# Layer 1's V in four second-level products instead of seven, q's combinations on VectorE, q's averages in other tiles

## The chip, the cores and the metric

The kernel runs on one core of a Trainium2 chip. The metric is the device time of one execution in microseconds, as the median of several runs. All data are float32. TensorE (PE) multiplies into PSUM, VectorE (DVE) and ScalarE (ACT) read PSUM and SBUF, GpSimd (POOL) works on SBUF alone, and SyncE (SP) issues most of the transfers.

## The reference

Eight images of 512 channels and 32 x 32 positions (N = 1024) pass through two attention layers.

```python
# layer 0: group norm of 32 groups, 8 heads of 64
h = group_norm(x, norm_w, norm_b)
q, k, v = split_heads(einsum('oc,bchw->bohw', qkv_w, h) + qkv_b)
attn = softmax(einsum('bhnd,bhmd->bhnm', q, k) / sqrt(64))
x = x + einsum('oc,bchw->bohw', proj_w, heads(attn @ v)) + proj_b
# layer 1: norm over the whole image, one head of 512
n = (x - mean(x)) * rsqrt(var(x) + 1e-5) * gn_gamma + gn_beta
q, k, v = wq @ n + bq, wk @ n + bk, wv @ n + bv
attn = softmax(q.T @ k * 512**-0.5)
x = x + wo @ (v @ attn.T) + bo
```

In layer 1 the kernel folds wq with wk, and wv with wo, into single weights (`wqk1`, `wvo1`). It then computes one "q", to be multiplied with the image itself, and one "V" from the image itself. The change lies in these two products.

## The kernel before

**Strassen steps.** Nearly every matrix product is a Strassen step: the operands are cut into quarters (A11 to A22, B11 to B22), combinations of them (S1 to S4, T1 to T4) are formed, and seven products of half the size replace eight. The seven are (A11, B11), (A12, B21), (S1, T1), (S2, T2), (S3, T3), (A22, T4) and (S4, B22). A product can itself be cut a second time in the same way, into seven products of quarter size; its operands then need their own combinations, called "twice" in the code. `PAIRS` and `REST` name which first-level products are taken together in a bank: `PAIRS` holds (A12, B21), (S1, T1), (S4, B22) and (A22, T4), `REST` holds (A11, B11), (S2, T2) and (S3, T3).

**Two forms of a product.** `by_two_steps` cuts only the four products of `PAIRS` a second time. They run in 14 steps (0 to 13, two groups of seven in turn), and the three others follow as larger matmuls that accumulate in one bank, in six "line" steps (14 to 19). `seven_by_two_steps` cuts all seven: groups z (two products) and w (one) in 14 steps, some additions between results, then groups c and d (two products each) in 14 more, then more additions. Each step is a few matmuls into one bank of PSUM and one read of it, a copy on ScalarE where the result is fresh, an addition on VectorE where it isn't. A bank is written again some steps later, after its read.

**Which form is where.** In layer 1, q is cut in all seven in images 0 to 6 (`make_q_twice`), and V too (`make_v_all`, L1778, with the matmuls at L1786). In the last image, 7, q has a form of its own (`make_q`), and V is `make_v_twice` (L1047, matmuls at L1055, line steps through L783), which is `by_two_steps` with the four of `PAIRS`.

**Order.** The instruction orders of PE, ScalarE and VectorE are as written in the code (`manual_schedule`). GpSimd's and SP's queues are ordered by the framework from the order of the code and what is ready. Each queue runs in its order, so an instruction that waits holds all that is behind it. Work of other kinds is put between steps by `at_steps`: `hooks` and `hooks_v` map a step's number to what is issued after it, in q and in V.

**What stands at the hooks of q (images 0 to 6).** The norm of layer 1 is needed only at the end of q. `both_halves` is seven tiny GpSimd operations. `mean_of_all` (step 5) and `deviation` (step 9) each do a small matmul with `in_sample` (L305), which averages over the partitions, and write its result into half a PSUM tile that `room(name, 0)` takes from `spares[0]`, here the second bank of z's tile "o". VectorE reduces it (L307), and GpSimd or VectorE goes on. `untaken` and `bias` (step 12) are eight tiny operations on VectorE, and the additions at the end of the first half (L712) need them.

**What stands at the hooks of V.** `onto_first` (step 2) adds the bias to q's first quarter on ScalarE. `finish_q` (L1776) forms q's four combinations S1 to S4, eight adds of 128x512, and `halve_a("S1")` (L520) the four combinations of S1's quarters: in images 0 to 6 both on GpSimd at step 2, in image 7 on VectorE at steps 5, 7, 9, 11 and 17. `measure_later` are the statistics of the image after next (ScalarE, four operations each, from the tiles x_stat), at steps 14, 17, 19, 21 of q and then of V, and `both_halves` for them at step 26 of V. They exist in images 0 to 5.

**After V.** The scores stage (`line`, `twice`) multiplies q's parts with the image. It first forms further quarters (A12, S3, T3 on VectorE at its steps 2, 5, 8; S4 and A22 on GpSimd), and sums of V's quarters follow on GpSimd (L1963).

**Weights.** A weight's second-level combinations are computed once, in image 0, and stored in device memory (`make_twice`). `WeightTwice` loads them back for each image, one tile of up to 512 KB for each entry of `TWICE`. For `wvo1` there are four entries, 2, 2, 2 and 1 products.

Of the kernel before, what the change touches and what calls it, by code (L numbers as in the profile page):

```python
# [46 lines left out]
P = 128  # L47
# [18 lines left out]
def two_attention_blocks(  # L66
# [35 lines left out]
    def tile2(name):  # L102
        return tpool.tile([P, 2, HALF], FP, tag="t", name=name)
# [451 lines left out]
    PAIRS_Q = [[("A12", "B21"), ("S4", "B22")], [("S1", "T1"), ("A22", "T4")]]  # L555
    PAIRS = [[("A12", "B21"), ("S1", "T1")], [("S4", "B22"), ("A22", "T4")]]
    REST = [[("A11", "B11"), ("S2", "T2")], [("S3", "T3")]]
    TWICE = {"wqk1": PAIRS + REST, "wvo1": PAIRS + REST}

    class WeightTwice:  # L560

# [117 lines left out]
    def seven_by_two_steps(multiply, at, z, c, w, bias, name):  # L679

        def group(tag, products, use_of):
            line, single = (banks(t, f"ps_{t}{tag}_{name}") for t in "so")
            spares.append(single[:, 1, :])  # L690
            line, single = line[:, 0, :], single[:, 0, :]
            for bank, x, y, start, fresh, r, t in [
                (line, "A11", "B11", True, True, 0, 0), (single, "A12", "B21", True, False, 0, 0),
                (line, "S2", "T2", False, True, 0, 1), (single, "S1", "T1", True, True, 1, 1),
                (line, "S3", "T3", False, False, 1, 1), (single, "S4", "B22", False, False, 0, 1),
                (line, "A22", "T4", False, True, 1, 0),
            ]:
                multiply(bank, products, x, y, start)
                tiles, always = use_of
                to = at(tiles, r, t)  # L700
                of = bank[:, : len(products) * 2 * P].rearrange("p (i q) -> p i q", i=to.shape[1])
                if fresh and not always:
                    nc.scalar.copy(to, of)
                else:
                    nc.vector.tensor_tensor(to, of, to, ALU.add)
                yield

        def plus(to, x, y, by=None):
            if by is None:
                nc.vector.tensor_tensor(to, x, y, ALU.add)  # L710
            else:
                nc.vector.scalar_tensor_tensor(to, x, by, y, ALU.add, ALU.add)  # L712

        def in_order(order, **groups):
            for n in order:
                next(groups[n])
                yield

        spares.clear()
        first = dict(z=group("z", REST[0], (z, False)), w=group("w", REST[1], (w, False)))  # L720
        yield from in_order("zzwzwzwzwzwzww", **first)
        for k in range(2):
            plus(z[k][:, 1, :], z[k][:, 0, :], z[k][:, 1, :], bias and bias(k, 0))
        for k in range(2):
            plus(w[k], w[k], z[k][:, 1, :], bias and bias(k, 1))
        spares.clear()
        c_of, d_of = [("S1", "T1"), ("A22", "T4")], [("A12", "B21"), ("S4", "B22")]
        second = dict(c=group("c", c_of, (c, False)), d=group("d", d_of, (z, True)))
        yield from in_order("ccdcdcdcdcdcd", **second)
        next(second["d"])  # L730
        for k in [1, 0]:
            plus(z[k][:, 1, :], z[k][:, 1, :], c[k][:, 0, :])
        for k in range(2):
            both = w[k].unsqueeze(1).to_broadcast([P, 2, HALF])
            nc.gpsimd.tensor_tensor(c[k], c[k], both, ALU.add)
        yield
        spares.clear()
# [233 lines left out]
    def flat(t):  # L971
        return t.rearrange("p h n -> p (h n)")
# [71 lines left out]
    def columns_of(w):  # L1044
        return lambda i, name: w.parts[0][name][:, :, i * P : (i + 1) * P]
# [100 lines left out]
    def layer0(bs, qs, ks, vs, b, norm_next, ending, begun):  # L1146
# [69 lines left out]
        if b == 0:  # L1216
# [16 lines left out]
            hooks[7].append(p0.finish)  # L1233
            at_steps(together(*pairs_qk(w, 1, bs, qs, ks, b)), hooks)
            steps = []
            for name, ns in [("v0", range(2)), ("p0", range(2)), ("wqk1", range(4)), ("wvo1", range(2, 4))]:
                of = [columns_of(of) for of in waiting if of.name == name]
                steps += make_twice(name, ns, of[0] if of else None)
            for n, step in enumerate(steps):
                at_units.setdefault(3 + 3 * n // 2, []).append(step)  # L1240
        else:
            ps[0], = begun
            accs[units[0][:2]] = ps[0]
# [321 lines left out]
    def attention1(xs, norm, ready, b, at_values, norms):  # L1565
# [170 lines left out]
            (of["A11"], of["A21"]), (of["A12"], of["A22"]) = ([halves(t) for t in ts] for ts in qs)  # L1736
        else:
            hooks = {
                0: [norm.both_halves], 5: [norm.mean_of_all], 9: [norm.deviation],
                12: [norm.untaken, lambda: biases.append(norm.bias())],  # L1740
                16: [lambda: twice_w.append(WeightTwice("wvo1"))],
            }
            if b + 2 < B:
                later = []

                def load_later(i):
                    if not i:
                        norms[b + 2] = norm0([later, None], b + 2)
                    norms[b + 2].xs[i] = [tile2(f"x_{b + 2}_{i}{half}_stat") for half in range(2)]
                    for half in range(2):  # L1750
                        nc.sync.dma_start(norms[b + 2].xs[i][half], quarter_of(x, b + 2, i, half))

                def measure_later(n):
                    norms[b + 2].moments(n // 2, n % 2, n % 2 == 0)

                for i in range(2):
                    hooks.setdefault(10 * i, []).append(lambda i=i: load_later(i))
                for n in range(4):
                    hooks.setdefault([14, 17, 19, 21][n], []).append(lambda n=n: measure_later(n))
                    hooks_v.setdefault([14, 17, 19, 21][n], []).append(lambda n=n: measure_later(n + 4))  # L1760
                hooks_v[26] = [lambda: norms[b + 2].both_halves()]
                at_values[5] = [lambda: norms[b + 2].mean_of_all()]
                at_values[7] = [lambda: norms[b + 2].deviation()]
            at_steps(make_q_twice(w), hooks)
# [1 line left out]

        w = next_weight("wvo1")

        def finish_q(n, engine):
            of[f"S{n}"] = halves(tile2(f"s{n}_q_{b}"))  # L1770
            x, y, op = {
                1: ("A21", "A22", ALU.add), 2: ("S1", "A11", ALU.subtract),
                3: ("A11", "A21", ALU.subtract), 4: ("A12", "S2", ALU.subtract),
            }[n]
            for k in range(2):
                engine.tensor_tensor(of[f"S{n}"][k], of[x][k], of[y][k], op)  # L1776

        def make_v_all(w):  # L1778


            parts = twice_w[0].all(columns_of(w))

            def multiply(bank, products, x, y, start):
                for i, (a, v) in enumerate(products):
                    for u in range(2):
                        nc.tensor.matmul(  # L1786
                            bank[:, (2 * i + u) * P : (2 * i + u + 1) * P],
                            twice_b[v][y][:, u * P : (u + 1) * P], parts[a][x],
                            start=start and i == u == 0, stop=True, skip_group_check=True,
                        )  # L1790

            def at(tiles, r, t):
                both = tiles[t] if len(tiles[t].shape) == 2 else flat(tiles[t])
                return both.rearrange("p (m o) -> p m o", o=2 * P)[:, :, r * P : (r + 1) * P]

            z, c = ([tile2(f"{n}_v_1_{b}_{t}") for t in range(2)] for n in "zc")
            u = halves(tile2(f"w_v_1_{b}"))
            v_of.update({
                (0, 0): [t[:, 0, :] for t in z], (1, 0): [t[:, 1, :] for t in z],
                (0, 1): [t[:, 0, :] for t in c], (1, 1): [t[:, 1, :] for t in c],  # L1800
            })
            return seven_by_two_steps(multiply, at, z, c, u, None, f"v_1_{b}")

        v_of = {}
        if last:
            v_pairs = places_v(f"1_{b}")
            for n in range(1, 5):
                hooks_v.setdefault(2 * n + 3, []).append(lambda n=n: finish_q(n, nc.vector))
            hooks_v[17] = [lambda: halve_a("S1")]
            at_steps(make_v_twice(w, twice_w[0], bs, twice_b, v_pairs, f"v_1_{b}"), hooks_v)  # L1810
            v_of.update({(n, i): [t[:, i, :] for t in v_pairs[n]] for n in range(2) for i in range(2)})
        else:
            for n in range(1, 5):
                hooks_v[2].append(lambda n=n: finish_q(n, nc.gpsimd))
            hooks_v[2].append(lambda: halve_a("S1", None, nc.gpsimd))
            at_steps(make_v_all(w), hooks_v)


        ps = [[[tile2(f"p_1_{b}_{j}{k}{i}") for i in range(2)] for k in range(2)] for j in range(2)]
# [103 lines left out]
        def halve_t3():  # L1923
# [12 lines left out]
        halve_a("S4", None, nc.gpsimd)  # L1936
        halve_a("A22", None, nc.gpsimd)
        svs = {f"S{n}": tile2(f"s{n}_v_1_{b}") for n in range(1, 5)}
        quarter_v = [
            [[t.rearrange("p (u o) -> p u o", u=2) for t in v_of[n, i]] for i in range(2)] for n in range(2)  # L1940
        ]
        v_parts = [
            {
# [763 lines left out]
```

## Time and profile before

| | before |
|---|---|
| median of 3 runs | 2817.36 us (2816.91 to 2820.29) |
| profiled execution | 2814.56 us |
| its span, first to last instruction | 2812.1 us |
| one image (first matmul of V in image 0 to that in image 1: 342.21 to 686.71) | 344.5 us |
| granted TensorE clock | 0.999 |

The profile is of one execution. Groups are by source line, engine, operation and tiles, with count, busy time, mean duration and the idle time of the engine before them. PE is the matmul part of TensorE, PEld its weight loads, which overlap. In the list of stretches each row gives the stretch, its length, the busy time of each engine with the count of its instructions in brackets, the granted clock, the share of DMA and GB/s. In the lists in order of time each row gives the start, the time to the end of the row's last instruction, the engine, the line and the tiles, and in square brackets the idle time before with what ended it.

### The profile page before, as it was taken

The page shows a single profiled execution, that of the slowest core. Times are in us where ns is not written, and L with a number is a line of the kernel's source. Part 1 is how long each engine was busy: PE and PEld are TensorE (multiplying, and loading weights), DVE is VectorE, ACT ScalarE, POOL GpSimd, SP SyncE. Part 2 cuts the span into 40 slices and gives each one's busy share as a digit, 9 for nine tenths or more (in the row PEclk, how much of TensorE's full clock was granted, in tenths as well). Part 3 has the DMA queues.
Part 4 walks back from the last instruction along what each step waited for, and adds up shares of the span by engine and source line. Part 5 has one row for each costly group of instructions (what it writes and reads, how often), then busy time and mean ns, then how long its engine had stood idle before and what let it go on. Part 6 is the DMA issues. An engine that isn't in the chain of part 4 may idle for free.

```text
span 2812.1 us, 42413 instructions
## 1 busy us (share of the span) xinstructions
PE 2771.6 (99%) x16570; PEld 1648.4 (59%) x16570; DVE 2197.6 (78%) x2993; ACT 1197.3 (43%) x1939; POOL 741.0 (26%) x710
## 2 busy tenths in 40 slices
PE   9999999999999999999999999999999999999999
PEld 5437774377643776437764477645676356763375
DVE  6787687876878768887688877877778877788877
ACT  3453443625346153462535524255342653326622
POOL 0001470015600265002640036400463005520021
PEclk9999999999999999999999999999999999999999
DMA  7555513255142551326422264322633236240101
GB/s 256 198 145 198 217 57 139 58 207 194 57 139 58 210 191 65 135 62 229 165 103 96 76 226 153 123 84 70 239 139 139 69 92 240 86 168 30 36 27 39
DMA packets 117552, 366.50 MB, mean 130 GB/s; under 512 B 25388, under 2 KB 26188, under 8 KB 110944
## 3 DMA queue, kind: packets, MB, share of 16 engines
q1 hardware_dynamic: 90576, 301.26, 31.1%
q10 hardware_dynamic: 26768, 62.46, 6.7%
q8 instruction: 132, 2.16, 0.3%
q14 instruction: 76, 0.62, 0.1%
HBM read 259.85 MB, written 79.99 MB: 121 GB/s over the span
## 4 chain that ended last, share of the span: by engine, by line
PE 93%; DVE 3%; issue 2%; DMA 1%; ACT 0%; ACTq 0%; SPq 0%; POOL 0%; DVEq 0%; POOLq 0%
PE ps_o L1185 15%; PE s L1136 14%; PE ps_o L2025 10%; PE ps_l L1860 5%; PE ps_l_qk L1034 5%; PE ps_s L1843 4%; PE ps_s L1860 4%; PE ps_s_qk L1027 3%; PE ps_l_v L783 3%; PE ps_l_p L768 3%; PE ps_o_qk L1027 2%; PE ps_s_v L1055 2%; PE ps_s_p L1092 2%; PE ps_s_two L2155 2%; PE ps_o_v L1055 2%
## 5 line engine op out<-in xcount | busy, mean ns | idle before, releaser
L940 ACT ACTIVATE p<-s 128x1024 f32<-128x1024 f32 x505 | 516.2, 1024 | 310.2 <-PE s L1136 303.4
L942 DVE TENSOR_TENSOR acc<-acc,p 128x1024 f32<-128x1024 f32 x384 | 469.2, 1222 | 64.0 <-ACT p L940 55.7
L1136 PE MATMUL s<-qk_back,qk_back 64*64 64x512 f32 x3528 | 457.4, 590 | 0.0
L1185 PE MATMUL ps_o<-p,v_back 64*64 64x512 f32 x3528 | 455.3, 589 | 0.0
L537 POOL TENSOR_TENSOR B_twice_p<-o 128x512 f32<-128x512 f32 x14 | 20.9, 1494 | 1070.7 <-DVE o L1205 1070.7
L1185 PEld LDWEIGHTS ps_o<-p,v_back 64*64 64x64 f32 x3528 | 134.9, 133 | 243.6 <-issue 239.8
L1136 PEld LDWEIGHTS s<-qk_back,qk_back 64*64 64x64 f32 x3528 | 132.6, 133 | 245.6 <-issue 216.5
L2025 PE MATMUL ps_o<-t_p,s_v 128*128 128x512 f32 x384 | 169.6, 596 | 0.0
L1834 ACT ACTIVATE p<-p,factor 128x512 f32<-128x512 f32 (+1 forms) x112 | 84.5, 780 | 113.3 <-DVE p L1870 86.4
L537 POOL TENSOR_TENSOR B_twice<-x 128x512 f32<-128x512 f32 x23 | 35.6, 1549 | 358.6 <-DVE x L1447 177.2
L2025 PEld LDWEIGHTS ps_o<-t_p,s_v 128*128 128x128 f32 x384 | 71.8, 190 | 88.4 <-issue 88.0
L942 DVE TENSOR_TENSOR acc<-p,p 128x1024 f32<-128x1024 f32 x57 | 69.7, 1223 | 45.7 <-ACT p L940 45.7
L1870 DVE TENSOR_TENSOR p<-ps_l,p 128x512 f32<-128x512 f32 x136 | 91.5, 688 | 17.8 <-PE ps_l L1860 16.1
L1848 ACT COPY p<-ps_s 128x512 f32<-128x512 f32 x96 | 53.1, 588 | 114.3 <-PE ps_s L1843 114.3
L1034 PE MATMUL ps_l_qk<-t,w_qk 128*128 128x512 f32 x224 | 100.3, 595 | 0.3
L641 ACT COPY c_q<-ps_s_qk 128x512 f32<-128x512 f32 x56 | 32.7, 583 | 140.7 <-PE ps_s_qk L1027 140.7
L373 POOL TENSOR_TENSOR rstd<-rstd,minus_half 128x4 f32<-128x4 f32 (+1 forms) x16 | 12.9, 806 | 285.0 <-DVE rstd L372 285.0
L1831 POOL TENSOR_TENSOR acc<-acc,p 128x512 f32<-128x512 f32 x48 | 83.5, 1740 | 13.3 <-ACT p L1834 10.8
L1870 DVE TENSOR_TENSOR p<-ps_s,p 128x512 f32<-128x512 f32 x112 | 74.7, 684 | 7.8 <-PE ps_s L1860 7.7
L1034 PEld LDWEIGHTS ps_l_qk<-t,w_qk 128*128 128x128 f32 x224 | 42.0, 190 | 56.3 <-issue 50.2
L661 DVE SCALAR_TENSOR_TENSOR c_q<-ps_l_qk,vec,c_q 128x512 f32<-128x512 f32 x56 | 40.8, 749 | 34.2 <-PE ps_l_qk L1034 33.8
L659 DVE TENSOR_TENSOR c_v<-ps_l_v,c_v 128x512 f32<-128x512 f32 x64 | 42.7, 689 | 31.3 <-PE ps_l_v L783 31.2
(780 smaller groups left out, 6077.0 us busy)
## 6 DMA issues: line engine op xcount, KB each, us to landing
x<-in_x SPq DMA_DIRECT2D x64, 512.0 KB, 9.2
qk_back<-kept_qk SPq DMA_DIRECT2D x56, 512.0 KB, 6.2
w_qk<-stored_qk SPq DMA_DIRECT2D x14, 1792.0 KB, 8.6
fold<-acc SPq DMA_DIRECT2D x56, 256.0 KB, 3.0
qk_twice<-stored_qk_twice ACTq DMA_DIRECT2D x28, 512.0 KB
kept_v<-c_v SPq DMA_DIRECT2D x28, 512.0 KB
kept_qk<-c_q SPq DMA_DIRECT2D x28, 512.0 KB, 3.3
kept_qk<-c_k SPq DMA_DIRECT2D x28, 512.0 KB, 3.5
```

What stands on the lines that cost most here:

```text
L940: nc.scalar.activation(p, s, AF.Exp, scale=factor)
L942: nc.vector.tensor_tensor(acc, first, p, ALU.add)
L1027: nc.tensor.matmul(bank[:, i * 2 * P : (i + 1) * 2 * P], parts[a][x], twice_b[v][y], start=start and i == 0, stop=True, skip_group_check=True,
L1034: nc.tensor.matmul(bank, of(i, a)[:, k, :], bs[v][:, k, :], start=start and k == 0, stop=k == 1, skip_group_check=True,)
L1055: nc.tensor.matmul(bank[:, (2 * i + u) * P : (2 * i + u + 1) * P], twice_b[v][y][:, u * P : (u + 1) * P], parts[a][x], start=start and i = ...
L1136: nc.tensor.matmul(s[cols, j, :], ks[pair][k0 // HALF][rows, k0 % HALF : k0 % HALF + HD], qs[pair][g][rows, :], start=True, stop=True,)
L1185: nc.tensor.matmul(o[cols, half, :], vs[n][kt % 4 // 2][rows, h, c0 : c0 + HD], p[rows, j, :], start=kt == 0, stop=kt == NT - 1,)
L1834: nc.scalar.activation(p, p, AF.Exp, scale=norm.factor)
L1843: nc.tensor.matmul(bank, bs[v][:, k, t * P : (t + 1) * P], of[a][k], start=a == "A11" and k == 0, stop=k == 1, skip_group_check=True,)
L1860: nc.tensor.matmul(bank[:, u * 2 * P : (u + 1) * 2 * P], v[y][:, u * P : (u + 1) * P], a[x], start=start and u == 0, stop=True, skip_group ...
L1870: nc.vector.tensor_tensor(at(r, t), bank, at(r, t), ALU.add)
L2025: nc.tensor.matmul(bank, v_parts[kt // 2][a][:, kt % 2, c * P : (c + 1) * P], p_parts[kt // 2][b][:, kt % 2, cols], start=fresh and kt == ...
```

## The change

V takes one form in all images: `make_v_all` goes, and `make_v_twice` runs with the four products of `PAIRS`. q stays with all seven. `wvo1` loses its `REST` combinations: they are no longer computed in image 0, nor loaded. The steps that compute stored combinations in image 0 are spaced two units apart instead of one and a half.

q's combinations S1 to S4 are formed by VectorE in all images, in images 0 to 6 after steps 7, 9, 11 and 13 of V, and S1's quarters by VectorE after step 15. The statistics in V move from steps 14, 17, 19, 21 (of 28) to 5, 8, 11, 14 (of 20), and their `both_halves` to step 17.

In q, `spares` now holds two half tiles for each group, in the order z's "o", z's "s", w's "o", w's "s". The mean moves from step 5 to step 7 and goes into w's "s"; the deviation moves from step 9 to step 11 and stays in z's "o"; `untaken` and `bias` move from 12 to 13.

```diff
-    TWICE = {"wqk1": PAIRS + REST, "wvo1": PAIRS + REST}
+    TWICE = {"wqk1": PAIRS + REST}
...
         def group(tag, products, use_of):
             line, single = (banks(t, f"ps_{t}{tag}_{name}") for t in "so")
-            spares.append(single[:, 1, :])
+            spares.extend([single[:, 1, :], line[:, 1, :]])
...
-            for name, ns in [("v0", range(2)), ("p0", range(2)), ("wqk1", range(4)), ("wvo1", range(2, 4))]:
+            for name, ns in [("v0", range(2)), ("p0", range(2)), ("wqk1", range(4))]:
...
-                at_units.setdefault(3 + 3 * n // 2, []).append(step)
+                at_units.setdefault(3 + 2 * n, []).append(step)
...
             hooks = {
-                0: [norm.both_halves], 5: [norm.mean_of_all], 9: [norm.deviation],
-                12: [norm.untaken, lambda: biases.append(norm.bias())],
+                0: [norm.both_halves], 6: [lambda: spares.insert(0, spares[3])], 7: [norm.mean_of_all],
+                10: [lambda: spares.pop(0)], 11: [norm.deviation],
+                13: [norm.untaken, lambda: biases.append(norm.bias())],
                 16: [lambda: twice_w.append(WeightTwice("wvo1"))],
...
-                    hooks_v.setdefault([14, 17, 19, 21][n], []).append(lambda n=n: measure_later(n + 4))
-                hooks_v[26] = [lambda: norms[b + 2].both_halves()]
+                    hooks_v.setdefault([5, 8, 11, 14][n], []).append(lambda n=n: measure_later(n + 4))
+                hooks_v[17] = [lambda: norms[b + 2].both_halves()]
...
-        def finish_q(n, engine):
+        def finish_q(n):
...
             for k in range(2):
-                engine.tensor_tensor(of[f"S{n}"][k], of[x][k], of[y][k], op)
-
-        def make_v_all(w):
...
-        if last:
-            v_pairs = places_v(f"1_{b}")
-            for n in range(1, 5):
-                hooks_v.setdefault(2 * n + 3, []).append(lambda n=n: finish_q(n, nc.vector))
-            hooks_v[17] = [lambda: halve_a("S1")]
-            at_steps(make_v_twice(w, twice_w[0], bs, twice_b, v_pairs, f"v_1_{b}"), hooks_v)
...
-        else:
-            for n in range(1, 5):
-                hooks_v[2].append(lambda n=n: finish_q(n, nc.gpsimd))
-            hooks_v[2].append(lambda: halve_a("S1", None, nc.gpsimd))
-            at_steps(make_v_all(w), hooks_v)
+                nc.vector.tensor_tensor(of[f"S{n}"][k], of[x][k], of[y][k], op)
+
+        v_pairs = places_v(f"1_{b}")
+        for n in range(1, 5):
+            hooks_v.setdefault(2 * n + (3 if last else 5), []).append(lambda n=n: finish_q(n))
+        hooks_v.setdefault(17 if last else 15, []).append(lambda: halve_a("S1"))
+        at_steps(make_v_twice(w, twice_w[0], bs, twice_b, v_pairs, f"v_1_{b}"), hooks_v)
```

More of the change, by code (lines that the diff above doesn't have):

```diff
@@ L1775, in finish_q @@
             for k in range(2):
-                engine.tensor_tensor(of[f"S{n}"][k], of[x][k], of[y][k], op)
-        def make_v_all(w):
[L1781 to L1802, printed above, removed]
@@ L1804, in attention1 @@
-        v_of = {}
-        if last:
-            v_pairs = places_v(f"1_{b}")
-            for n in range(1, 5):
-                hooks_v.setdefault(2 * n + 3, []).append(lambda n=n: finish_q(n, nc.vector))
-            hooks_v[17] = [lambda: halve_a("S1")]
-            at_steps(make_v_twice(w, twice_w[0], bs, twice_b, v_pairs, f"v_1_{b}"), hooks_v)
-            v_of.update({(n, i): [t[:, i, :] for t in v_pairs[n]] for n in range(2) for i in range(2)})
-        else:
-            for n in range(1, 5):
-                hooks_v[2].append(lambda n=n: finish_q(n, nc.gpsimd))
-            hooks_v[2].append(lambda: halve_a("S1", None, nc.gpsimd))
-            at_steps(make_v_all(w), hooks_v)
+                nc.vector.tensor_tensor(of[f"S{n}"][k], of[x][k], of[y][k], op)
@@ L1938, in attention1, with halves_of @@
         svs = {f"S{n}": tile2(f"s{n}_v_1_{b}") for n in range(1, 5)}
+        def halves_of(n, i):
+            return [t[:, i, :] for t in v_pairs[n]]
         quarter_v = [
-            [[t.rearrange("p (u o) -> p u o", u=2) for t in v_of[n, i]] for i in range(2)] for n in range(2)
+            [[t.rearrange("p (u o) -> p u o", u=2) for t in halves_of(n, i)] for i in range(2)] for n in range(2)
         ]
```

## The prediction

> **What bounds the kernel now.** I read the page first, then what TensorE (PE) waited for, then the stretches of layer 1 in image 0 beside those of the last image, then the instructions in order of time.
>
> ```profile
> PE 2771.6 (99%) x16570; PEld 1648.4 (59%) x16570; DVE 2197.6 (78%) x2993; ACT 1197.3 (43%) x1939; POOL 741.0 (26%) x710
> ```
>
> PE is busy for 2771.6 of 2812.1 us, so there are two ways to gain: less PE work, or fewer of the 40 us in which PE stands. The list of PE's waits says where those are.
>
> ```profile
> PE ps_oc_v L1786 <- DVE c_v L705: 18.9, 7, 2.7
> PE ps_oz_q L305 <- DVE z_q L705: 6.1, 7, 0.9
> PE ps_oz_q L305 <- ACT z_q L703: 5.4, 7, 0.8
> ```
>
> Columns: us in total, times, longest. All three occur once in each of images 0 to 6, and all lie in stages that the change touches: the first in V, the others at the two averages inside q. The stretches (span, then busy us by engine): q, V and scores of image 0, then V and scores of image 7, which already runs the code that images 0 to 6 are given.
>
> ```profile
> 318.03:342.21 24.18, 22.41 (x103) 18.74 (x102) 14.97 (x32) 11.90 (x28) 3.77 (x13) 1.00 0.89 326
> 342.21:367.11 24.90, 22.20 (x197) 22.00 (x196) 17.77 (x23) 13.04 (x30) 20.75 (x21) 1.00 0.21 75
> 367.11:411.39 44.28, 44.28 (x175) 32.52 (x174) 39.44 (x49) 17.79 (x28) 31.63 (x26) 1.00 0.17 60
> 2690.80:2713.67 22.87, 22.87 (x161) 21.63 (x160) 18.14 (x33) 4.68 (x8) 6.29 (x8) 1.00 0.00 1
> 2713.67:2757.62 43.95, 43.95 (x173) 32.68 (x172) 32.99 (x48) 17.99 (x28) 11.18 (x8) 1.00 0.00 1
> ```
>
> The reader is to see that V with four products twice (22.87 us) has more PE work than V with seven (22.20 busy) and is still shorter than it (24.90), for it has no hole. Where the hole comes from, image 0 in order of time (VectorE, GpSimd, PE):
>
> ```profile
> 351.69 3.28 DVE L710 TENSOR_TENSOR z_v<-z_v 128x512 f32<-128x512 f32 x2
> 354.89 3.43 DVE L710 TENSOR_TENSOR w_v<-w_v,z_v 128x512 f32<-128x512 f32 x2
> 358.24 0.68 DVE L705 TENSOR_TENSOR c_v<-ps_oc_v,c_v 128x512 f32<-128x512 f32 x1
> ...
> 354.38 3.39 POOL L1776 TENSOR_TENSOR s_q<-z_q 128x512 f32<-128x512 f32 x2
> ...
> 358.97 1.16 PE L1786 MATMUL ps_oc_v<-wvo_twice,T_twice 128*128 128x128 f32 x8 [2.71 <-DVE c_v L705]
> ```
>
> The four L710 adds of V take 6.7 us while GpSimd forms q's combinations; the same two-operand line takes 1.29 us for two in q (343.21), when GpSimd is idle. The read of ps_oc_v stands behind them, and PE behind that read.
>
> [...] 3.28 against 1.29 us above, while VectorE's adds with one PSUM input keep 0.68 us beside the same GpSimd work. [...]
>
> **The change part by part**, per image, images 0 to 6.
>
> *V's matmuls.* Removed: 98 matmuls of 128 columns. The trace has two PE instructions for each and 8 in 0.893 us (352.53 to 353.42), so 196 x 0.1117 = 21.9 us. Added: 56 of that kind (12.5) and 24 of 256 columns (48 x 0.2158 = 10.4): 22.87, which is what image 7 measures. Cost +1.0 us of work; the hole of 2.7 and some 0.3 us of small change go. V without a new wait: 22.87 - 24.90 = **-2.03 us**.
>
> *q's combinations to VectorE.* Eight adds of 128x512; in image 7 they cost 1.28 us for two. GpSimd loses 12 us and the S1 quarters. VectorE loses in V the four L710 adds and one z += c pair (8 us). Does VectorE stay ahead of PE? Offsets from V's start, 0.893 us a step for steps 0 to 13, then 1.727. S1 (step 7) needs c_q += w_q on GpSimd, which ends at 349.05, offset 6.84: S1 is done by about 8.1, and the next read of a bank is due at 8.2. S2, S3, S4 behind steps 9, 11, 13 end at 11.0, 13.5, 14.7. Covered by PE: nothing.
>
> *ScalarE.* The second half of the statistics moves from steps 14 to 21 of 27 to steps 5 to 14 of 20: 1.73 us each, between copies of 0.58. Copy 6 then ends at offset 8.4, and PE writes that bank again at 8.93; copy 7 at 8.9 against 9.82. Tight, covered. Their data is there: SP issued those four loads by 324.4 and they land in 9.6 us.
>
> *S1's quarters, step 15.* This is the weak place. Image 7 has them at step 17 and with GpSimd just idle again; here they come ahead of the read for step 16, which PE needs at step 18 (offset 19.42). Adds of steps 14 and 15 end near 17.1. GpSimd takes S4's and A22's quarters as soon as S4 is there (in image 7 at 2704.44, 0.2 us after it), here from 14.7, or from 16.7 behind the seven tiny operations of the statistics, for 6.5 us or more. The same four quarters with GpSimd idle (image 7) and beside just those GpSimd quarters (image 0):
>
> ```profile
> 2711.03 0.41 DVE L520 TENSOR_TENSOR S_twice<-s_q 128x256 f32<-128x256 f32 x1
> 2711.48 0.42 DVE L520 TENSOR_TENSOR S_twice<-S_twice,s_q 128x256 f32<-128x256 f32 x1
> ...
> 376.45 0.41 DVE L520 TENSOR_TENSOR spare<-s_q 128x256 f32<-128x256 f32 x1
> 376.89 0.83 DVE L520 TENSOR_TENSOR spare<-spare,s_q 128x256 f32<-128x256 f32 x1
> 377.65 0.94 DVE L520 TENSOR_TENSOR spare<-s_q 128x256 f32<-128x256 f32 x1
> 378.52 0.94 DVE L520 TENSOR_TENSOR spare<-s_q,spare 128x256 f32<-128x256 f32 x1
> ```
>
> So 1.5 us against 2.9. Undisturbed: 17.1 + 1.5 + 0.7 (the read) = 19.3 to 19.5, PE waits 0.1 at most. Disturbed: 17.3 to 17.6 + 2.9 + 0.7 = 20.9 to 21.2, PE waits **1.5 us** at step 18. I take that; bounds 0.1 and 2.6 (other adds in steps 13 to 15 slowed as well). V: -2.03 + 1.5 = **-0.5 us**.
>
> *q's averages.* Before, each writes into the tile that the step just ahead of it filled, and waits for that tile's reader. From 321.91 + 0.43 to 323.49, and from 326.16 to 327.42, PE spends 1.15 and 1.26 us, 2.57 with the slower start behind each; in image 7 an average costs 0.14 + 0.09. After, the first goes into w's score tile, read one step earlier (PE gets there 1.29 us after step 5's end, ScalarE's second copy ends at 1.15), the second into z's other tile, read two steps earlier. The spread on GpSimd needs 1.6 us from the first average, and four steps give 2.6. Gain 2.57 - 0.46 = 2.1. But the deviation now comes only two steps ahead of the second group: untaken waits for GpSimd's power and begins some 0.4 us later against PE, and behind it stands the read that PE already waits for at ps_oc_q (0.3 us, the hole ahead of 334.34). Hence **-1.7 us**; bounds -2.1 and -0.9 (one average still waiting).
>
> *Scores.* GpSimd has no c_v += w_v (5.2 us) after V, VectorE no z += c: 44.28 falls towards image 7's 43.95. Taken **-0.3**, bounds 0 and -0.33.
>
> *Edits at nothing.* Two loads (768 KB) fewer per image on ScalarE's queue, and in image 0 twelve adds of 0.28 us, three loads, two stores and a wider spacing of such steps: layer 0 is hidden behind PE, which is busy 107.77 of 107.77 us in units of image 1; uncovered, 3.4 us once. SP's weight loads keep their releasers; fewer buffers are held, so no tile comes free later.
>
> **Sum.** -0.5 - 1.7 - 0.3 = -2.5 us (2.53 unrounded) x 7 = -17.7 us. The profiled execution took 2814.56 us, so 2796.9; the median of the runs shown lies 2.8 above it, which gives 2799.7.
>
> **Rivals.**
> A (the forecast): both holes go, S1's quarters cost 1.5 us. 2799.7. Against it: GpSimd's order there is not in the trace.
> B: GpSimd's quarters miss S1's (they come earlier, or later because of order: in image 0 they stood behind c_v += w_v although S4 was there). -2.03 + 0.1 - 1.7 - 0.33 = -3.96 x 7: 2789.6.
> C, slower: S1's quarters block behind long GpSimd instructions. The row of spare<-c_q,c_q has 2574 ns for one quarter beside a 128x1024 GpSimd add, and spare<-spare,c_q 2454. With two such and two of 0.94 the four last 6.9 us, PE waits about 5.5 at step 18: V +3.5, q -1.7, sum +1.8 x 7 = +12.6: 2830.0. It decides from a halving of 5.2 us on (a wait of 3.7 eats V's 2.03 and q's 1.7). Against it: those long adds should be over at offset 6.84.
> D: VectorE is late in both stages: q -0.9, V +0.4 (a wait of 2.4), scores 0: -0.5 x 7 = -3.5: 2813.9.
>
> **How the numbers follow.** A 0.52, B 0.25, D 0.15, C 0.08. Of D I count 0.05 as faster, 0.10 as within 0.2% (5.6 us, what a measurement of this kernel can tell). Faster 0.82, same 0.10, slower 0.08. The range holds A with its bounds and B, and leaves out C and most of D: 2787 to 2813.
>
> **What would show it.** PE's waits without ps_oc_v and without the two at L305; V near 24.4 us, with a hole of 1.5 just ahead of the last two line steps, released by VectorE's add onto c_v, and S1's quarters at 0.8 to 0.9 us just before it. V at 22.9 means B. A wait on ScalarE's copies at steps 10 or 11 would say that the statistics were moved too early; holes over 3.7 us in V, or a longer q, that the forecast is wrong.

## The result, and the profile after

The changed kernel takes 2797.93 us (median of 4 runs, 2797.44 to 2798.8) against 2817.14 us before (4 runs, 2813.59 to 2820.29): a ratio of 0.9933, 95% interval 0.9915 to 0.995. The forecast was 2799.7. Its profiled span is 2797.1 us, 15.0 less than before.

The page, engines:

```profile
PE 2772.4 (99%) x16318; PEld 1645.5 (59%) x16318; DVE 2147.5 (77%) x3023; ACT 1186.7 (42%) x1911; POOL 598.2 (21%) x612
```

PE is busy for 0.8 us more than before, and GpSimd for 143 us less. So all of the gain lies in time in which PE stood, that is, waited with nothing to do. (The page counts a matmul at a lower clock as busy for as long as it takes: in the profile before PE is busy for all of the 3.41 us from 179.64 with 20 matmuls, at a clock of 0.50, and for all of the next 3.41 us with 36, at 1.00.) PE's waits (total, times, longest):

```profile
PE ps_l_v L783 <- DVE c_v L659: 9.3, 7, 1.4
PE ps_oc_q L1697 <- DVE c_q L705: 2.6, 7, 0.4
PE ps_l_qk L1034 <- DVE c_k L661: 2.1, 2, 1.4
PE ps_sum L1315 <- DVE acc L1307: 1.4, 1, 1.4
...
PE ps_sc_q L1697 <- ACT c_q L703: 0.7, 1, 0.7
```

The three waits shown of before are gone. In place of V's 18.9 us stand 9.3 us at the line steps, and nothing at L305. q, V and scores of image 0 after the change, as stretches:

```profile
316.17:338.41 22.24, 21.87 (x104) 18.92 (x103) 14.78 (x32) 11.90 (x28) 3.16 (x12) 1.00 0.86 319
338.41:363.16 24.75, 23.38 (x162) 21.54 (x161) 19.03 (x30) 11.55 (x26) 14.09 (x18) 1.00 0.21 75
363.16:407.30 44.14, 44.14 (x173) 32.59 (x172) 31.58 (x47) 17.79 (x28) 17.90 (x16) 1.00 0.18 62
```

So q went from 24.18 to 22.24, V from 24.90 to 24.75, scores from 44.28 to 44.14. Nearly all of the gain per image is q's. V kept its length although its old hole went, for a new one stands in it. In order of time, image 0, VectorE, GpSimd and PE:

```profile
355.57 0.78 DVE L520 TENSOR_TENSOR S_twice<-s_q 128x256 f32<-128x256 f32 x1
356.38 0.83 DVE L520 TENSOR_TENSOR S_twice<-S_twice,s_q 128x256 f32<-128x256 f32 x1
357.14 0.94 DVE L520 TENSOR_TENSOR S_twice<-s_q 128x256 f32<-128x256 f32 x1
358.00 0.94 DVE L520 TENSOR_TENSOR S_twice<-s_q,S_twice 128x256 f32<-128x256 f32 x1
358.87 1.27 DVE L659 TENSOR_TENSOR c_v<-ps_l_v,c_v 128x512 f32<-128x512 f32 x2
...
355.34 1.59 POOL L520 TENSOR_TENSOR S_twice<-s_q 128x256 f32<-128x256 f32 x2
356.89 0.90 POOL L520 TENSOR_TENSOR S_twice<-S_twice,s_q 128x256 f32<-128x256 f32 x1
357.76 0.90 POOL L520 TENSOR_TENSOR A_twice<-c_q,c_q 128x256 f32<-128x256 f32 x1
...
359.60 3.72 PE L783 MATMUL ps_l_v<-w_wvo,t 128*128 128x256 f32 x16 [1.37 <-DVE c_v L659]
```

This is the order that the forecast assumed: GpSimd's S4 and A22 quarters begin 0.2 us before S1's on VectorE, both engines slow down (a quarter takes 0.78 to 0.94 us on VectorE, 0.41 where GpSimd is idle, and 0.90 on GpSimd, 0.72 once VectorE's are over), the two reads of the bank stand behind them, and PE waits 1.37 us behind the first read.

Over seven images, by stage lengths: q -12.4 us, V -2.7 (1.4 of it in image 5 alone, see the last section), scores -0.8. Outside them, layer 0 of image 0 is 2.6 shorter. A new wait at L1034 (ps_l_qk) gives back 1.3 in image 4 and 0.7 in image 0. That makes -16.5; VectorE's last operation is 16.7 us earlier. The end of the kernel behind it is 1.7 longer in this profile. That end takes 4.2 to 6.0 us in the twelve profiles, and what sets it was not followed up.

### The profile page after: what moved, and what is told of

It reads as the page before. It is cut to its first block, busy times and chain, and to the rows that moved or that the text cites. A ratio compares the mean times of both kernels' runs of the same rounds, so it can differ in the third digit from the quotient of the medians.

```text
span 2797.1 us, 41715 instructions
## 1 busy us (share of the span) xinstructions
PE 2772.4 (99%) x16318; PEld 1645.5 (59%) x16318; DVE 2147.5 (77%) x3023; ACT 1186.7 (42%) x1911; POOL 598.2 (21%) x612
## 4 chain that ended last, share of the span: by engine, by line
PE 91%; DVE 5%; POOL 1%; issue 1%; ACT 1%; DMA 1%; ACTq 0%; SPq 0%; DVEq 0%; POOLq 0%
PE ps_o L1185 15%; PE s L1136 15%; PE ps_o L1995 10%; PE ps_l L1827 5%; PE ps_l_qk L1034 5%; PE ps_s L1810 4%; PE ps_l_v L783 4%; PE ps_s L1827 4%; PE ps_s_qk L1027 3%; PE ps_l_p L768 3%; PE ps_o_qk L1027 2%; PE ps_s_v L1055 2%; PE ps_s_p L1092 2%; PE ps_s_two L2125 2%; PE ps_o_v L1055 2%; PE ps_o_two L2125 1%
## 5 line engine op out<-in xcount | busy, mean ns | idle before, releaser
L659 DVE TENSOR_TENSOR c_v<-ps_l_v,c_v 128x512 f32<-128x512 f32 x120 | 79.2, 686 | 44.8 <-PE ps_l_v L783 44.7
L1034 PE MATMUL ps_l_qk<-t,w_qk 128*128 128x512 f32 x224 | 100.3, 595 | 2.3 <-DVE c_k L661 2.1
L641 ACT COPY c_v<-ps_s_v 128x512 f32<-128x512 f32 x90 | 52.7, 585 | 91.1 <-PE ps_s_v L1055 91.1
L1034 PEld LDWEIGHTS ps_l_qk<-t,w_qk 128*128 128x128 f32 x224 | 42.0, 190 | 58.3 <-issue 50.2
```

What stands on the lines that cost most here:

```text
L1034: nc.tensor.matmul(bank, of(i, a)[:, k, :], bs[v][:, k, :], start=start and k == 0, stop=k == 1, skip_group_check=True,)
```

## The experiments

All were compared with the kernel before; the edits are against the changed kernel unless said otherwise.

### S1's quarters two steps later

```diff
-        hooks_v.setdefault(17 if last else 15, []).append(lambda: halve_a("S1"))
+        hooks_v.setdefault(17, []).append(lambda: halve_a("S1"))
```

> The changed kernel with one edit: S1's quarters stand after step 17 of V, behind both reads that PE's last two line steps need, instead of after step 15. Theory (VectorE's quarters of S1 are slowed by GpSimd's quarters and hold the read that step 18 needs): the wait of PE at ps_l_v (9.3 us in total, 1.4 each, some 1.7 with the slower starts) goes, the quarters themselves stay slow (about 0.9 each), V takes 22.9 to 23.1 us, and the kernel 7 x 1.4 to 1.7 less than the changed one: 2786 to 2788. Rival (VectorE has too much to do at V's end, so PE waits a little later): V falls to 22.9 but the first products of the scores stage wait for their bank by 1 us or more, and the time stays at 2795 to 2799.

Measured: 2787.38 us (2786.44 to 2787.71), ratio 0.9889, 0.9874 to 0.9904. V is 23.11 or 23.12 in all seven images, without a wait. VectorE in image 0:

```profile
359.12 0.69 DVE L659 TENSOR_TENSOR c_v<-ps_l_v,c_v 128x512 f32<-128x512 f32 x1 [1.03 <-PE ps_l_v L783]
359.73 0.90 DVE L520 TENSOR_TENSOR S_twice<-s_q 128x256 f32<-128x256 f32 x1
360.67 0.83 DVE L520 TENSOR_TENSOR S_twice<-S_twice,s_q 128x256 f32<-128x256 f32 x1
361.42 0.94 DVE L520 TENSOR_TENSOR S_twice<-s_q 128x256 f32<-128x256 f32 x1
```

Three of the quarters are as slow as before the edit, but the read that PE needs is now ahead of them. The place costs, not the slowness by itself. One number of a hook is worth 1.64 us of V in images 0 to 5 and 1.28 in image 6. The median falls by 10.5 us, more than half of what all of the change brought.

### S1's quarters on GpSimd

```diff
-        hooks_v.setdefault(17 if last else 15, []).append(lambda: halve_a("S1"))
+        if last:
+            hooks_v.setdefault(17, []).append(lambda: halve_a("S1"))
+        else:
+            hooks_v[7].append(lambda: halve_a("S1", None, nc.gpsimd))
```

> The changed kernel with one edit: in images 0 to 6 S1's quarters are formed by GpSimd, behind step 7, as soon as S1 is there and in GpSimd's idle stretch before the statistics; VectorE has none of them. Theory: no wait at ps_l_v, V 22.9 to 23.1 us, 2786 to 2788; S2's two adds on VectorE may be slowed from 1.3 to 2.2 us by GpSimd, which is covered. Rival (whatever GpSimd does in V costs VectorE and so PE): a wait of 0.5 us or more at the banks of steps 10 to 12 instead, 2791 to 2798.

Measured: 2791.08 us (2790.74 to 2791.51), ratio 0.9902, 0.9887 to 0.9918; V 23.81. That is some two thirds of what the first experiment gained. PE's wait in V, and VectorE's adds of S2 in image 0:

```profile
PE ps_l_v L783 <- DVE c_v L659: 3.4, 7, 0.5
```
```profile
349.33 1.97 DVE L1777 TENSOR_TENSOR s_q<-s_q,z_q 128x512 f32<-128x512 f32 x2
```

These two adds take 1.28 us in the first experiment. They now meet GpSimd's S1 quarters and lose 0.7 us. VectorE has no pause between them and the line steps, so it is still late there, and PE waits 0.5 us. The expectation had the slower adds right but took them to be covered. The contention moved with the work.

### No quarters on GpSimd beside V

S4's and A22's quarters go to VectorE, after steps 9 and 10 of scores (images 0 to 6).

```diff
+                **({} if last else {9: [lambda: halve_a("S4")], 10: [lambda: halve_a("A22")]}),
...
-        halve_a("S4", None, nc.gpsimd)
-        halve_a("A22", None, nc.gpsimd)
+        if last:
+            halve_a("S4", None, nc.gpsimd)
+            halve_a("A22", None, nc.gpsimd)
```

> The changed kernel with one edit: in images 0 to 6 the quarters of S4 and A22, which GpSimd forms while VectorE forms S1's, are formed by VectorE in the scores stage (after its steps 9 and 10). S1's quarters stay on VectorE after step 15. Theory [...]: the four fall from 3.3 to 1.5 us, the wait at ps_l_v from 1.4 to at most 0.2 us, 2786 to 2790. Rival (the place alone: VectorE is behind there whatever GpSimd does): the four still last 1.5 at best but the wait stays above 1 us, 2796 to 2799; or the work moved into the scores stage makes PE wait there.

Measured: 2799.09 us (2798.19 to 2799.75), ratio 0.9931, 0.9918 to 0.9945. VectorE in V of image 0, with S1's quarters still after step 15:

```profile
355.18 0.41 DVE L520 TENSOR_TENSOR S_twice<-s_q 128x256 f32<-128x256 f32 x1
355.62 0.43 DVE L520 TENSOR_TENSOR S_twice<-S_twice,s_q 128x256 f32<-128x256 f32 x1
355.96 0.42 DVE L520 TENSOR_TENSOR S_twice<-s_q 128x256 f32<-128x256 f32 x1
356.30 0.41 DVE L520 TENSOR_TENSOR S_twice<-s_q,S_twice 128x256 f32<-128x256 f32 x1
```

The same four stand at the same place and take 0.41 to 0.43 us each, and V is 23.11 without a wait (23.13 in image 6). So it was GpSimd's quarters that slowed them. The time comes back one stage later: scores are 45.95 us instead of 44.14, for there PE now waits on VectorE, which has the quarters to do as well:

```profile
PE ps_l L1827 <- DVE p L1837: 11.4, 7, 1.6
```

### The averages alone, and undone

The kernel before with only the change's edits to `spares`, `mean_of_all`, `deviation` and `untaken`; and the changed kernel with those four undone.

```diff
-            spares.append(single[:, 1, :])
+            spares.extend([single[:, 1, :], line[:, 1, :]])
...
-                0: [norm.both_halves], 5: [norm.mean_of_all], 9: [norm.deviation],
-                12: [norm.untaken, lambda: biases.append(norm.bias())],
+                0: [norm.both_halves], 6: [lambda: spares.insert(0, spares[3])], 7: [norm.mean_of_all],
+                10: [lambda: spares.pop(0)], 11: [norm.deviation],
+                13: [norm.untaken, lambda: biases.append(norm.bias())],
```

> The kernel before with one edit: q's averages as the change has them (other tiles, steps 7 and 11 instead of 5 and 9, the tiny operations at 13). V with all seven, q's combinations on GpSimd, as before. Theory: the two waits at L305 go, the wait at ps_oc_q grows to about 0.4 us, q falls from 24.2 to 22.2 us, V stays 24.9: 7 x 1.9 = 13.5 us less than before, 2803 to 2805. Rival (PE's waits in q only move, since VectorE's end of q is what sets V's hole): q gains the same but V's wait grows by as much, 2811 or more.

> The changed kernel with q's averages as before (z's tile, steps 5 and 9, the tiny operations at 12). Theory (the averages are worth what q lost, 12.4 us in the two profiles, and nothing else depends on them): both waits at L305 are back, q 24.2 us, V and scores as in the changed kernel, ScalarE no longer waits for x_stat: 2797.9 + 12.4 = 2810, with 2808 to 2811 as the bounds. Rival (with the averages alone the kernel before gained only 4.6 us, so they are worth that here too, and the rest is V's): 2801 to 2804.

Undone: 2811.56 us (2810.87 to 2812.7), ratio 0.9978, 0.9969 to 0.9987. q is 24.18 in every image, both waits at L305 are back. By medians the averages are worth 13.6 us in the changed kernel (12.1 by the two profiled spans), and the rest of the change 5.8.

Alone: 2812.72 us (2810.13 to 2818.39), ratio 0.9986, 0.9979 to 0.9994: a miss. q is 22.24 to 24.17, on the mean only some 1 us shorter than before. The waits at L305 are gone, but there is another; waits, then ScalarE and PE in image 2 in order of time:

```profile
PE ps_sc_q L1697 <- ACT c_q L703: 4.5, 5, 1.4
```
```profile
1019.51 0.63 ACT L333 ACTIVATE mean<-x_stat 128x512 f32<-128x512 f32 x1 [2.77 <-DMA x_stat<-in_x]
...
1022.81 1.13 PE L1697 MATMUL ps_sc_q<-T_twice,wqk_twice 128*128 128x256 f32 x4 [0.87 <-ACT c_q L703]
```

ScalarE comes to q's statistics (after step 14) earlier than before, and the tile has not landed. It waits 15.1 us in all in that profile for x_stat, where it did not wait before, and its copies of q's banks stand behind. The second cause is that V's hole stayed, with what follows it: V is 5.0 us longer in sum than in the profile before (last section).

### The statistics of q later

In the changed kernel, and in the kernel before with the averages alone.

```diff
-                    hooks.setdefault([14, 17, 19, 21][n], []).append(lambda n=n: measure_later(n))
+                    hooks.setdefault([18, 20, 22, 24][n], []).append(lambda n=n: measure_later(n))
```

> The changed kernel with the statistics in q after steps 18, 20, 22, 24 instead of 14, 17, 19, 21; those in V stay. Theory (q is now short enough for ScalarE to reach the statistics before x_stat has landed, and the copies that PE needs stand behind it): ScalarE's waits for x_stat, 14.7 us in total, fall below 4, the wait of PE at ps_sc_q goes, q is 22.2 to 22.3 in every image; 0.8 to 1.5 us less than the changed kernel, 2796.4 to 2797.2. Rival (the late statistics push ScalarE's work into V, whose copies come late at steps 4 to 7): V longer by 0.3 us or more, 2798 to 2801.

> The kernel before with the change's averages in q, and q's statistics after its steps 18, 20, 22 and 24 instead of 14, 17, 19 and 21. Theory: the averages alone brought about 7 of 13.5 us since ScalarE reached the statistics before x_stat had landed; with the later steps q is 22.25 in all seven images, no wait at ps_sc_q, 13.5 us less in q. V keeps its hole of 2.7 us, and behind it the clock falls in one to four of the seven images, 1.5 us each, so the median is 2803 to 2808. Rival: another wait takes its place (q above 22.4 in several images), or the load is late at those steps too, and the median stays at 2810 to 2813.

The averages alone with late statistics: 2805.82 us (2805.62 to 2811.24), ratio 0.9958, 0.9944 to 0.9971. q is 22.24 in all seven images, and no wait for x_stat is left. That settles the first cause of the miss. In the changed kernel, late statistics give 2797.86 us (2796.99 to 2798.61), ratio 0.9927, 0.9914 to 0.9941. In the profile of the changed kernel the wait had cost 1.2 us, in image 1 alone (q 23.44). It is gone, and q is 22.24 to 22.26 in all images. The median, only 0.07 us lower, does not show it.

### Layer 0 of image 0

The forecast counted the edits there at nothing, and layer 0 became 2.6 us shorter. PE of the kernel before, then of the changed one:

```profile
175.44 1.06 PE L1315 MATMUL ps_sum<-acc,ones 64*32 64x512 f32 x8
178.82 1.17 PE L1315 MATMUL ps_sum<-acc,ones 64*32 64x512 f32 x8 [2.31 <-DVE acc L1307]
179.92 1.98 PE L1136 MATMUL s<-q,k 64*64 64x512 f32 x8
```
```profile
175.43 1.06 PE L1315 MATMUL ps_sum<-acc,ones 64*32 64x512 f32 x8
177.85 1.06 PE L1315 MATMUL ps_sum<-acc,ones 64*32 64x512 f32 x8 [1.37 <-DVE acc L1307]
178.85 1.09 PE L1136 MATMUL s<-q,k 64*64 64x512 f32 x8
```

Both kernels are level at 175.4. Before, PE waits 0.94 us longer, and behind the longer hole the granted clock is 0.50 from 179.64 to 183.05: eight matmuls take 1.98 us instead of 1.09. Half speed for 3.41 us loses some 1.7 us, which with the 0.94 makes the 2.6. VectorE of the kernel before, ahead of that wait's end:

```profile
176.61 0.28 DVE L520 TENSOR_TENSOR wqk_twice<-again_wqk 128x128 f32<-128x128 f32 x1
...
177.54 1.22 DVE L1307 TENSOR_TENSOR acc<-acc,fold 128x1024 f32<-128x1024 f32 x1
```

The add at L1307 stands behind four adds of stored combinations. After the change it begins at 176.58. Two experiments: the changed kernel with wvo1's REST combinations computed and loaded again (nothing uses them) at the old spacing, and the kernel before with the new spacing alone.

```diff
-    TWICE = {"wqk1": PAIRS + REST}
+    TWICE = {"wqk1": PAIRS + REST, "wvo1": PAIRS + REST}
...
-                at_units.setdefault(3 + 2 * n, []).append(step)
+                at_units.setdefault(3 + 3 * n // 2, []).append(step)
```

> The changed kernel with image 0's work on wvo1 put back: the three further products' combinations are computed and stored again, with the old spacing of one and a half units, and loaded again for each image (nothing uses them). Theory (that work made VectorE late at the end of layer 0 of image 0, where the sum over the keys waits for it): layer 0 of image 0 ends 2.6 us later, the wait at ps_sum (L1315) goes from 1.4 back to 2.3 us or more, the rest stays: 2800 to 2801. Rival (the 2.6 us came from somewhere else, or the two loads per image matter): no change, or more than 3 us, since the loads come in front of x_stat or behind it in each image.

> The kernel before with one edit: the steps that compute stored combinations in image 0 stand two units apart instead of one and a half, all of them still there. Theory: in layer 0 of image 0 four such adds on VectorE stood ahead of the add at L1307 and made PE's wait at L1315 2.3 us long, and behind it the clock fell to 0.70; with the spacing alone they come behind that add, the wait is 1.4 us, the clock stays at 1.00 there, and the first V matmul of layer 1's weights at L1055 comes at 223.6 to 224.5 instead of 226.24. Everything else as before: q 24.18, V 24.90 or 26.3 where the clock falls behind its hole. Median 2814 to 2816 against 2817.3. Rival: the 2.6 us belong to the computing of wvo1's REST combinations, which is still here: the wait at L1315 stays at 2.3 and the median at 2817.

REST back, with the old spacing: 2801.98 us (2800.1 to 2802.83), ratio 0.9942, 0.9929 to 0.9956. The four adds stand ahead of L1307 again, which begins at 177.86. But PE came to its wait 0.96 us later in this profile, for a reason that lies further ahead and stays open. So the hole is 1.7, the clock stays at 1.00, and layer 0 of image 0 ends at 224.92 (the first matmul at L1055 behind it; 223.64 in the changed kernel, 226.24 before). With both edits back, half of the 2.6 us is back. q is 2.0 us longer over the seven images, with PE's waits at ps_sc_q in two of them. Whether the loads that are back cause that is not shown: ScalarE waits 12.0 us for x_stat here and 14.7 in the changed kernel.

Spacing alone: 2818.45 us (2814.83 to 2821.89), ratio 1.0004, 0.9996 to 1.0012: nothing. Its waits:

```profile
PE ps_o_v L1055 <- DVE o L1192: 2.3, 1, 2.3
PE ps_sum L1315 <- DVE acc L1307: 1.4, 1, 1.4
```

The wait at L1315 is 1.4, and the first matmul at L1055 comes at 223.87 instead of 226.24, as the theory had it. But the REST adds now stand as late as 219.62, VectorE is behind at the end of layer 0, and PE waits 2.3 us on it five microseconds later. So the spacing is what shortens the wait at L1315, but alone it brings nothing in sum; without the REST work it can be wide and not reach the end of layer 0. Dropping REST alone, at the old spacing, was not run. It comes last in the list of these steps, so it could hardly move the four adds of `wqk1`, but that is argued.

### What the runs point to

S1's quarters after step 17, late statistics, and the deviation one step earlier in w's tile "o".

```diff
-                10: [lambda: spares.pop(0)], 11: [norm.deviation],
-                13: [norm.untaken, lambda: biases.append(norm.bias())],
+                9: [lambda: spares.__setitem__(0, spares[3])], 10: [norm.deviation],
+                12: [norm.untaken, lambda: biases.append(norm.bias())],
```

> The changed kernel with three edits: S1's quarters after step 17, the statistics in q after 18, 20, 22, 24, and q's deviation after step 10 in w's tile o, with the tiny operations after 12 (so GpSimd's power is there 0.8 us earlier and VectorE reaches the read of ps_oc_q earlier). Theory: V 23.1 us, no wait at ps_oc_q and ps_sc_q, q 21.7 to 21.9 us: 10.5 from the first edit, 1 from the second, 3 to 4 from the third: 2782.5 to 2784. Rival (the deviation waits for the spread from GpSimd, so PE stands 0.3 to 0.5 us at L305 instead, and the third edit brings nothing): q 22.2, 2786 to 2787.

Measured: 2785.36 us (2785.13 to 2785.73), ratio 0.9883, 0.9868 to 0.9898, the best of all. PE's waits, and V of image 0 as a stretch:

```profile
PE ps_l_qk L1034 <- DVE c_k L661: 2.1, 2, 1.4
PE ps_sum L1315 <- DVE acc L1307: 1.4, 1, 1.4
PE ps_warm L2182 <- POOL in_sample L164: 1.2, 1, 1.2
```
```profile
337.92:361.02 23.10, 23.10 (x161) 21.70 (x161) 17.18 (x28) 11.55 (x26) 13.58 (x17) 1.00 0.22 80
```

PE does not stand in V any more. Against the first experiment q is 2.0 us shorter in sum, which is also what the medians differ by: the late statistics pay here. The deviation's edit brought nothing. It cut the wait at ps_oc_q from 0.37 to 0.12, yet q is 22.26, no shorter. The weights of the average at L305 now wait 0.3 us for GpSimd's spread, and the matmuls behind it begin 0.2 us later, as the rival had it.

## Why the prediction was right, and where it was off

**V: wait right, sum 0.38 us too good.** The wait of 1.5 at step 18 is there with 1.37 us, by the named cause, and the first and third experiments show it from both sides. V without the wait was put at 22.87, from image 7; it is 23.11 in images 0 to 6. With 1.64 lost around the wait, V is 24.75 and gains 0.15 where -0.53 was forecast. The term taken from another image is what was off, by 0.24, and the time lost around the wait by 0.14. In the last experiment's trace 0.14 of the 0.24 lies at V's start: the first and the third group of four matmuls take 0.55 and 0.49 us to the next group instead of image 7's 0.45, for their banks wait for the last reads of q's (ScalarE's c_q at L703, VectorE's z_q at L705).

**q's averages: right, 0.24 us too small.** -1.94 against -1.7 (-1.77 on the mean, as image 1 lost 1.2). The 0.4 us put against it for a later read at ps_oc_q did not come: that wait is 0.37, where 0.3 was read before.

**Scores: right sign, under half the size.** -0.14 in image 0 and -0.12 on the mean, against -0.3 taken.

**Edits at nothing: wrong once.** The step said that layer 0 is hidden behind PE, from a stretch of image 1, where PE never stands. In image 0 it stood once, at L1315, on VectorE's queue, and the half clock behind that hole more than doubled its price; that is 2.6 us of the result. "Uncovered, 3.4 us once" was its bound, but it had the twelve REST adds in mind; the four that stood ahead of L1307 belong to `wqk1`.

**Not in the prediction.** That a shorter q brings ScalarE to q's statistics before their load has landed. The prediction weighed the data of V's statistics, which moved, not those of q, which did not move but whose surroundings did. In the changed kernel that costs 1.2 us in the profile, and with the averages alone about half of their gain. Nor was the wait at L1034 foreseen (2.1 us in all), whose cause was not tried.

Summed, q -12.4, V -2.7 and scores -0.8 make -16.0 us, against -17.7 forecast; layer 0 adds -2.6, and the wait at L1034 takes back 2.0. Of V's 2.7, the half clock in one image of the profile before is 1.4, which no term had.

**That it lay so near is in part luck.** To the 2796.9 us for the profiled execution the forecast added 2.8, by which the median lay above the profile before. The last section has what the runs show of it: of 20 runs of the kernel before in one session, 17 have a mean granted clock below the profiled one's 0.999. That this is for the most part half clock behind V's hole, in more images than in the profiled one, is an estimate from the profiles of the other kernels with that hole, which have it in 4, 4 and 6 of 7 images. The change takes the hole away, and the excess is gone too: all four runs are at 0.999 or 1.000, the profiled execution takes 2798.8 us and the median is 0.9 below it. From profile to profile the forecast was 1.9 us too low, with the 2.8 added it was 1.8 too high for the median. The mechanisms hold, but the closeness of the number does not measure them.

One reading was loose. At 343.21 GpSimd was not idle all through VectorE's two adds: its own add at L735 begins at 343.98. The 1.28 us in image 7 is the same time for two such adds.

Of the rivals, B (V at 22.9, no contention) is excluded by the wait of 1.37 us in V. The first experiment comes close to its time, 2787.38 against 2789.6; it was one hook away. C and D are excluded by the stage lengths: the four quarters took 0.78 to 0.94 us each, not the 2.5 of C's long ones, and q was not late.

## What to carry to other kernels

Before work moves onto an in-order queue, list what stands right behind it: the same four slow adds cost 1.6 us an image ahead of a read that PE needs, and nothing behind it. When a stage gets shorter, check every load that was timed by its old length, not only the steps that move. And a hole in TensorE can cost more than its length (V's of 2.7 us cost 1.4 more in image 5 of the profile before, where the granted clock was 0.50 behind it), so the long holes go first.

## What the runs showed that was not expected

**The clock behind a hole.** V of image 5 of the kernel before is 26.26 us where the others are 24.90. The hole of 2.7 us is the same in every image, but in image 5 the granted clock (the third number from the end) falls to half behind it, which costs 1.4 us more than the hole. Stretches of 3.41 us, cut at the clock's own steps, around the hole of image 4 and then of image 5:

```profile
1732.70:1736.12 3.42, 1.51 (x14) 1.32 (x12) 3.42 (x3) 2.05 (x6) 3.42 (x3) 1.00 0.00 0
1736.12:1739.53 3.41, 2.61 (x23) 2.61 (x24) 2.56 (x5) 1.38 (x4) 3.41 (x4) 1.00 0.00 0
...
2077.45:2080.86 3.41, 1.25 (x12) 1.06 (x10) 3.41 (x3) 2.02 (x5) 3.41 (x3) 1.00 0.00 0
2080.86:2084.28 3.42, 2.88 (x13) 2.88 (x14) 1.78 (x3) 0.76 (x2) 3.42 (x4) 0.50 0.00 0
2084.28:2087.69 3.41, 3.41 (x33) 3.41 (x32) 2.24 (x4) 2.80 (x8) 2.47 (x8) 1.00 0.00 0
```

The clock changes at 179.64, 183.05, 2080.86 and 2084.28 in this trace, which are whole multiples of 3.413 us apart. So it is in all twelve traces, with the steps at other offsets in each run. Cut the twelve traces at these steps, leaving out their first 8 and last 15 us. In 18 stretches PE stood for 2.01 us or more, and behind each of them the clock is 0.50. In all others it stood for 1.91 us or less, and behind none of them does the clock fall. In image 4 a step cuts the hole into 1.91 and 0.80 us, in image 5 into 2.17 and 0.54. So the same hole costs more or not by where the steps fall, and in these traces the limit lies between 1.91 and 2.01 of the 3.41 us.

That gives half clock in 1 of 7 images (before), 4 of 7 (averages alone), 4 of 7 (before with the new spacing; one image lost 2.9 us, the clock staying down for 6.83) and 6 of 7 (averages with late statistics), one profile of each. The other three of the 18 lie behind the hole at L1315, of 2.3 to 2.9 us, in three of these four kernels. The hole of 2.25 us at L1055 in the kernel with the new spacing is cut into 0.92 and 1.33, and the clock stayed at 1.00 behind it, as it did behind all holes of 1.4 to 1.7 us.

It fits the spreads too: the four kernels with V's hole range over 5.6 to 10.0 us (5 to 20 runs in a session), those without it over 0.6 to 2.7 us (4 to 11 runs). And each run's mean granted clock goes with its time: of 20 runs of the kernel before in one session the three at 0.999 took 2813.6 to 2814.3 us, the four at 0.995 and 0.996 took 2820.1 to 2823.5, and after the change all four are at 0.999 or 1.000. The profile before, at 0.999, is one of the fast ones, 2.6 us below its median. That is most of why the gain by medians (19.2 us) is larger than by the two profiles (15.0).

**Contention on both sides.** Beside each other, quarters take 0.78 to 0.94 us on VectorE and 0.90 on GpSimd; with none on the other engine they take 0.41 and 0.72. So in such a row of short operations both engines lose, and VectorE's time about doubles.
